# Turning and spreading the softmax sums by DMA instead of by small matrix products

## The chip, the cores and the metric

The kernel runs on one core of one Trainium2 chip. The metric is the device time of one execution in microseconds (us), lower is better. The core has a matrix engine (PE; its weight loads are listed as PEld), a vector engine (DVE), an activation engine (ACT), a general engine (POOL) and a sequencer (SP) that here issues nearly all the DMAs. Each engine executes its own instructions strictly in the order in which they were written, and waits on semaphores where it needs another engine's or a transfer's result.

## The reference, cut to what matters

Four layers are applied in turn to 4 images of 128 channels and 64 x 64 pixels, each with a group norm before it and a residual after it: self-attention, a 5x5 convolution, a two-directional selective scan (a state-space layer), and a 3x3 convolution. Only the attention is changed here:

```python
q = jnp.einsum('bnc,dc->bnd', xt, Wq) + bq
k = jnp.einsum('bnc,dc->bnd', xt, Wk) + bk
v = jnp.einsum('bnc,dc->bnd', xt, Wv) + bv
scores = jnp.einsum('bic,bjc->bij', q, k) * scale
attn = jax.nn.softmax(scores, axis=-1)
out = jnp.einsum('bij,bjc->bic', attn, v)
```

All of it is in f32. There are 4096 queries and 4096 keys to an image.

## The kernel before, in words

**Tiling of the attention.** `attention` (one image) holds the scores with keys on partitions and queries along the row. It takes 8 blocks of 512 queries (`NM`), and for each block 32 tiles of 128 keys (`NJT`): 256 steps u. Step u makes one score product (`scores`, L482), which ACT exponentiates into a ring of 8 slots (L488), and the value product of step u - 2 (`values`, L494), which accumulates 128 channels x 512 queries in a PSUM bank. An f32 product is two records in the profile. The softmax is normalised afterwards: each query's sum over all keys is needed, inverted, and then laid out 128 x 512, the same row on every partition, so that `settle` can multiply the raw output by it, add it to the residual and take the statistics of the next norm.

**The sums of a block.** In the images 1 to 3 (`sums`, L516) PE adds four ring slots at a time, each against a 128x32 block of ones in its own quarter of the PSUM bank "z"; ACT copies the bank out (`evict_sums`, L542). In image 0, which runs alone, PE makes no such products: DVE and POOL add the even and the odd tiles into two 128x512 tiles (`side_sums`, L536). ACT copies out the raw output (`evict`, L547).

**What is done with them.** Four functions follow, put into later steps by `after(u, n, f, blk)`. `turn` (L559), one step later, brings the sums of 512 queries from one row to a 128x4 column form by PE products with a one-column right side: four products where ACT's copy is the source, eight where the two side tiles are. `invert`, at 2 steps, copies the 128x4 to `zall` (which a check of range reads at the end) and takes the reciprocal on DVE (L568, L570). `widen_out`, at 4 steps, spreads the 128x4 to 128x512 by four products with the identity (`spread`, L474) into the bank "z". `settle`, at 5 steps, multiplies and adds on DVE (L582, L583) and has ACT take the squares (L331). The last block of an image does the same four at once, after the loop.

**The scan and its order.** The selective scan is cut into 1024 ticks, 256 to an image (`scan_core`). In each tick POOL makes the drive `db` (L1258, 128x1024); ACT exponentiates the decay `da` (L1251); DVE runs the recurrence (L1268) in two halves of 512 or in one of 1024; the weighting by `cr` is made by DVE (L1271) or, for two ticks in five while attention runs, by POOL (L1289); and PE collects the finished ticks by 128x32 products (L1309). SP loads `br`, `cr` (L1234) and every 32 ticks `de`, `dx` (L1228) four ticks ahead, into three buffers of each.

**How the two are woven.** Everything else is one long generator, `images`: the attention, the convolution and the scan's preparation of images 0, 1, 2, 3, and then the last parts of images 0 to 3. Image 0's attention and convolution run alone, with the constants of the convolution beside them. From then on the generator is advanced by the scan's loop. Each `yield` of the generator gives its price: 0.86 (`PRODUCT`) for each 512-column PE product, and some small constants for steps without. A tick hands out `PACE` = 2.8 of credit, half of it at each of two points, and the generator runs until it is spent. `turn` and `widen_out` cost one `PRODUCT` each. Thus scan of image b and attention and convolution of image b + 1 are laid side by side, and the pace decides how much of the second stands between two ticks. If image b + 1 isn't prepared when the scan of image b is out of ticks, `before` runs the generator without ticks until it is. During the last image's scan the pace is 1.5 (`ENDPACE`).

The engines' programs come out of this weaving: each function's instructions, DMAs on SP among them, are written where the generator calls it.

Of the kernel before, what the change touches and what calls it, by code (L numbers as in the profile page):

```python
# [24 lines left out]
F32 = mybir.dt.float32  # L25
I32 = mybir.dt.int32
AF = mybir.ActivationFunctionType
ALU = mybir.AluOpType
AX = mybir.AxisListType
# [3 lines left out]
P = 128  # L33
# [3 lines left out]
MM = 512  # L37
# [5 lines left out]

PRODUCT, HOP, SLOT, PACE, ENDPACE, AHEAD = 0.86, 1.7, 0.7, 2.8, 1.5, 4


BQ, BK, BX, BP, CONVB, BD, DSKIP, MAINB, CONVW, ALOG = 0, 1, 2, 3, 4, 5, 6, 7, 8, 12
# [3 lines left out]
def conv_preact_kernel(  # L53
# [16 lines left out]
    nc = tc.nc  # L70
# [8 lines left out]
    NJT = L // P  # L79
    NM = L // MM  # L80
    TPM = MM // P
# [6 lines left out]
    small = ctx.enter_context(tc.tile_pool(name="small", bufs=2))  # L88
    dram = ctx.enter_context(tc.tile_pool(name="dram", bufs=2, space=DRAM))
    ps = ctx.enter_context(tc.tile_pool(name="ps", bufs=1, space=PSUM))  # L90
    pools, ready = {}, set()
    more = None

    def bank(tag, name):
        return pools.get(tag, ps).tile([P, MM], F32, tag=tag, name=name)
# [22 lines left out]
    ones = const.tile([P, P], F32, name="ones")  # L118
# [52 lines left out]
    zall = const.tile([P, B * NJT], F32, name="zall")  # L171
# [265 lines left out]
    def attention(b, xs, xn, v, st, safe, loads):  # L437
# [3 lines left out]
        rq, acc, zp, mb = {}, {}, {}, {}  # L441
        N = NM * NJT

        def after(u, n, f, *args):
            later.setdefault(u + n, []).append((f, args))

        def queries(blk):
            pr = bank("s", f"pr_{b}_{blk}")
            nc.tensor.matmul(pr, wqk, xn[:, bass.ts(blk, MM)], start=True, stop=True)
            rq[blk] = pools["bg"].tile([P, MM], F32, tag="r", name=f"r_{b}_{blk}")  # L450
            nc.scalar.activation(rq[blk], pr, AF.Identity, bias=bqk)

        def row_max(blk):

            part = small.tile([P, TPM, NM], F32, tag="part", name=f"part_{b}_{blk}")
            for t in range(TPM):
                for k in range(NM):
                    pp = bank("s", f"pmax_{b}_{blk}_{t}_{k}")
                    nc.tensor.matmul(
                        pp, rq[blk][:, bass.ts(t, P)], xn[:, bass.ts(k, MM)],  # L460
                        start=True, stop=True,
                    )
                    nc.vector.tensor_reduce(part[:, t, k : k + 1], pp, AX.X, ALU.max)
            m = small.tile([P, TPM], F32, tag="rmax", name=f"rmax_{b}_{blk}")
            nc.vector.tensor_reduce(m, part, AX.X, ALU.max)
            pb = bank("s", f"pmb_{b}_{blk}")
            spread(pb, m)
            mb[blk] = pools["bg"].tile([P, MM], F32, tag="w", bufs=4, name=f"mb_{b}_{blk}")
            nc.scalar.copy(mb[blk], pb)
# [9 lines left out]
        def scores(u):  # L479
            blk, j = divmod(u, NJT)  # L480
            sc = bank(("s", "s2")[u % 2], f"sc_{b}_{u}")
            nc.tensor.matmul(sc, xn[:, bass.ts(j, P)], rq[blk], start=True, stop=True)  # L482
            pt = ring[:, u % NRING, :]
            if safe:
                nc.vector.tensor_tensor(pt, sc, mb[blk], ALU.subtract)
                nc.scalar.activation(pt, pt, AF.Exp)
            else:
                nc.scalar.activation(pt, sc, AF.Exp)  # L488

        def values(u):  # L490
            blk, j = divmod(u, NJT)
            if j == 0:
                acc[blk] = bank("a", f"acc_{b}_{blk}")
            nc.tensor.matmul(  # L494
                acc[blk], v[:, j, :], ring[:, u % NRING, :], start=j == 0, stop=j == NJT - 1
            )
# [5 lines left out]
        def sums_due(u):  # L502
            beside = "collected" in ready
            ready.discard("collected")
            if due and due[0][1] <= u and (beside or u >= due[0][2]):
                sums(due.pop(0)[0])
                return PRODUCT
            return 0.0

        def sums(u):  # L510

            blk, j = divmod(u, NJT)
            if j == 3:
                zp[blk] = bank("z", f"zp_{b}_{blk}")
            for g in range(4):
                nc.tensor.matmul(  # L516
                    zp[blk][g * 32 : (g + 1) * 32, :], ones[:, :32],
                    ring[:, (u - 3 + g) % NRING, :], start=j == 3, stop=j == NJT - 1,
                    tile_position=(0, g * 32), skip_group_check=True,
                )  # L520

        state = {}


        fill = pools.get("fill") if not safe else None
        sides = {}

        def side_sums(u):
            blk, j = divmod(u, NJT)
            eng, e = (nc.vector, nc.gpsimd)[j % 2], "dp"[j % 2]  # L530
            if j < 2:
                sides[blk, e] = fill.tile([P, MM], F32, tag=f"side{e}", name=f"side{e}_{blk}")
                eng.tensor_copy(sides[blk, e], ring[:, u % NRING, :])
            else:
                s = sides[blk, e]
                eng.tensor_tensor(s, s, ring[:, u % NRING, :], ALU.add)  # L536

        def evict_sums(blk):
            zs = None
            if not fill:  # L540
                zs = pools["bg"].tile([P, MM], F32, tag="zs", bufs=1, name=f"zs_{b}_{blk}")
                nc.scalar.copy(zs, zp.pop(blk))  # L542
            state[blk] = None, zs

        def evict(blk):
            raw = pools["bg"].tile([P, MM], F32, tag="raw", bufs=1, name=f"raw_{b}_{blk}")
            nc.scalar.copy(raw, acc.pop(blk))  # L547
            state[blk] = raw, state[blk][1]
# [44 lines left out]
        for u in range(N):  # L593
            blk, j = divmod(u, NJT)
            cost = sums_due(u)
            if safe and j == 0:
                row_max(blk)
            scores(u)
            cost += PRODUCT

            if j == 17 and blk + 1 < NM:
                queries(blk + 1)
                cost += PRODUCT
            w = u - 2
            if w >= 0:
                if w < N - HELD:
                    values(w)
                    cost += PRODUCT
                d = w % NJT
                if fill:  # L610
                    side_sums(w)
                elif d == NJT - 1:
                    sums(w)
                    cost += PRODUCT
                elif d % 4 == 3:
                    due.append((w, u + (3 if d == 3 else 1), u + NRING - 5))
                if d == NJT - 1:
                    evict_sums(blk - 1)
                    evict(blk - 1)
                    for n, f in ((1, turn), (2, invert), (4, widen_out), (5, settle)):  # L620
                        after(u, n, f, blk - 1)
            for f, args in later.pop(u, ()):
                f(*args)
                cost += PRODUCT if f in (turn, widen_out) else 0.0
            next(loads, None)
            yield cost or HOP
        for w in (N - 2, N - 1) if fill else ():
            side_sums(w)
        blk = NM - 1
# [16 lines left out]
        if not fill:  # L646
            sums(N - 1)
            yield PRODUCT
        taps_to(NRING - 4)
        evict_sums(blk)  # L650
        values(N - 3)
        taps_to(NRING - 3)
# [727 lines left out]
    def program(safe):  # L1380
# [24 lines left out]
        def front(b, xn, v):  # L1405

            xs = large(b + 1, f"xs_{b}")[:, :L]
            st = Sums(f"e{b}")
            yield from attention(b, xs, xn, v, st, safe, load(xs, b))
            st2 = Sums(f"s{b}")  # L1410

            yield from conv_pairs(b, xs, f"A{b % 2}", st, st2, b > 0 or safe)
            if b + 1 == B:
                nc.sync.dma_start(m3, main_w)

            def mat(name):
                return dram.tile([NCH, P, CH], F32, tag=name, name=f"{name}_{b}")

            mats4[b] = (
                [mat("bm"), mat("cm")], mat("dd"), mat("dxd"), mat("xcd"),  # L1420
                dram.tile([P, L], F32, tag="xsd", bufs=B, name=f"xsd_{b}"),
            )
            ynds[b] = dram.tile([NM, P, MM], F32, tag="ynd", bufs=B, name=f"ynd_{b}")
            operands = yield from scan_prep(b, xs, st2, mats4[b])
            if b + 1 < B:
                return (yield from both(operands, start(b + 1, 10)))
            yield from operands
            last_weights()
# [225 lines left out]
```

## Time and profile before

| | |
|---|---|
| time, median of 3 (lowest to highest) | 4425.42 us (4424.64 to 4433.18) |
| span of the profiled execution | 4424.0 us |
| busy: PE, DVE, POOL, ACT | 3917.4, 3698.5, 3602.1, 2358.3 us |
| image 0's attention alone | about 30 to 490 us |
| image 0's convolution and scan preparation | about 490 to 684 us |
| scan of image 0 beside attention of image 1 | about 730 to 1363 us |
| scan of image 0 beside convolution, preparation of image 1 | about 1363 to 1633 us |
| the same for images 1 and 2 | 1664 to 2299 and on to 2572; 2609 to 3242 and on to 3511 us |
| scan of image 3 beside the last parts of images 0 to 2 | about 3511 to 4350 us |

The profiled execution's own time isn't recorded apart from its span, which is 1.4 us under the median of the timed runs, and 0.6 us under the fastest. In a table of stretches, each engine's figure is its busy time in that stretch with the count of its instructions in brackets, then the TensorE clock granted, the DMA share and the rate. In a group's line stand the code line, the engine, the operation, what it writes and reads, the count, then busy time in us and the mean of one in ns, then the idle time just before them and what ended it. A busy PE is not PE at its peak: ends of products are modelled, and a product that starts every 429 ns is shown as 592 ns long.

### The profile page before, as it was taken

What the parts mean: (1) busy time and instruction counts of PE and PEld (TensorE: products, weight loads), DVE (VectorE), ACT (ScalarE), POOL (GpSimd) and SP (SyncE); (2) the same over time, 40 slices, a digit from 0 to 9 for tenths busy, and PEclk for the clock granted to TensorE, in tenths of its full rate; (3) what the DMA queues carried; (4) which work ended last, traced back from release to release, by engine and by line L of the source; (5) the groups of instructions that cost most, each with busy time, mean ns of one, the idle gap of its engine ahead of it and who ended that gap; (6) DMA issues with size and microseconds to landing.
All of it is one profiled execution on the core that took longest, in us unless ns stands there. A gap on an engine that the chain in (4) does not pass through costs nothing. (4 is left out here: it accounts for less than half of the span.)

```text
span 4424.0 us, 43050 instructions
## 1 busy us (share of the span) xinstructions
PE 3917.4 (89%) x13480; PEld 1485.9 (34%) x13480; DVE 3698.5 (84%) x3472; ACT 2358.3 (53%) x4269; POOL 3602.1 (81%) x1713
## 2 busy tenths in 40 slices
PE   8999997999999979999989889999989748575667
PEld 4444433333333323333333333333333212121212
DVE  4722217999999989999999889999999899999996
ACT  3333217666665376666664576666653744454533
POOL 3433307999999978999999889999989889999995
PEclk9999999999999989999999989999999869787888
DMA  1000016545455566554544564454545665656562
GB/s 64 21 1 1 0 53 228 182 170 175 168 186 180 179 214 212 177 175 174 180 164 180 205 231 177 165 179 173 180 175 182 226 228 193 232 202 235 187 226 84
DMA packets 213167, 726.06 MB, mean 164 GB/s; under 512 B 25152, under 2 KB 26432, under 8 KB 212672
## 3 DMA queue, kind: packets, MB, share of 16 engines
q1 hardware_dynamic: 211328, 722.49, 46.3%
q8 instruction: 108, 1.77, 0.2%
q14 instruction: 131, 1.07, 0.1%
q10 hardware_dynamic: 1600, 0.73, 0.1%
HBM read 653.98 MB, written 69.14 MB: 163 GB/s over the span
## 5 line engine op out<-in xcount | busy, mean ns | idle before, releaser
L1258 POOL TENSOR_TENSOR db<-dx,br 128x1024 f32<-128x1024 f32 x1024 | 2398.1, 2365 | 223.8 <-DMA dx<-dxd 55.6
L1251 ACT ACTIVATE da<-de,a_neg 128x512 f32<-128x512 f32 (+1 forms) x1640 | 1302.4, 797 | 740.6 <-DVE da L1268 300.5
L482 PE MATMUL sc<-r,x 128*128 128x512 f32 x2048 | 1078.6, 609 | 14.8 <-ACT last L1284 6.9
L494 PE MATMUL acc<-exchange,v 128*128 128x512 f32 x2048 | 1048.3, 594 | 2.3
L1289 POOL TENSOR_TENSOR hc<-hc,cr 128x1024 f32<-128x1024 f32 x386 | 913.0, 2365 | 22.5 <-ACT last L1284 19.7
L1271 DVE TENSOR_TENSOR hc<-da,cr 128x512 f32<-128x512 f32 (+1 forms) x1003 | 839.6, 837 | 65.0 <-DVE da L1268 0.5
L1268 DVE TENSOR_TENSOR_SCAN da<-da,last,db 128x512 f32<-128x512 f32 (+1 forms) x480 | 863.1, 1798 | 24.3 <-POOL db L1258 12.1
L488 ACT ACTIVATE exchange<-sc 128x512 f32<-128x512 f32 x1024 | 603.5, 589 | 510.4 <-PE sc L482 503.9
L1309 PE MATMUL y<-hc,sel 128*32 128x512 f32 x4096 | 611.9, 647 | 270.6 <-POOL hc L1289 245.3
L482 PEld LDWEIGHTS sc<-r,x 128*128 128x128 f32 x2048 | 361.3, 190 | 585.6 <-issue 379.2
L494 PEld LDWEIGHTS acc<-exchange,v 128*128 128x128 f32 x2048 | 386.4, 190 | 499.2 <-issue 478.0
L1268 DVE TENSOR_TENSOR_SCAN hc<-da,last,db 128x512 f32<-128x512 f32 (+1 forms) x288 | 490.9, 1704 | 6.5 <-ACT da L1251 5.2
L1268 DVE TENSOR_TENSOR_SCAN da<-da,da,db 128x512 f32<-128x512 f32 x365 | 469.7, 1287 | 6.2 <-ACT da L1251 5.9
L536 POOL TENSOR_TENSOR sidep<-sidep,exchange 128x512 f32<-128x512 f32 x120 | 170.7, 1422 | 273.5 <-ACT exchange L488 271.3
L1268 DVE TENSOR_TENSOR_SCAN hc<-da,hc,db 128x512 f32<-128x512 f32 x251 | 322.0, 1283 | 35.6 <-ACT da L1251 11.8
L1309 PEld LDWEIGHTS y<-hc,sel 128*32 128x32 f32 x4096 | 114.4, 113 | 706.1 <-POOL hc L1289 337.7
L536 DVE TENSOR_TENSOR sided<-sided,exchange 128x512 f32<-128x512 f32 x120 | 95.9, 799 | 221.5 <-ACT exchange L488 220.1
L1268 DVE TENSOR_TENSOR_SCAN da<-da,db 128x512 f32<-128x512 f32 (+1 forms) x158 | 232.5, 1471 | 15.5 <-POOL db L1258 7.1
L698 PE MATMUL pcm<-xpm,cs 128*128 128x512 f32 x432 | 210.1, 635 | 23.1 <-ACT xpm L387 23.1
L964 PE MATMUL pe<-df,exchange 128*128 128x512 f32 x480 | 214.2, 595 | 0.0
L516 PE MATMUL zp<-exchange,ones 128*32 128x512 f32 x1536 | 204.9, 600 | 8.3 <-DVE xs L583 8.3
L1284 ACT COPY last<-da 128x1 f32<-128x1 f32 x474 | 73.8, 156 | 254.5 <-DVE hc L1271 252.0
(241 smaller groups left out, 2839.1 us busy)
## 6 DMA issues: line engine op xcount, KB each, us to landing
br<-bm SPq DMA_DIRECT2D x512, 512.0 KB, 5.2
cr<-cm SPq DMA_DIRECT2D x512, 512.0 KB, 3.9
de<-dd SPq DMA_DIRECT2D x64, 512.0 KB, 4.7
dx<-dxd SPq DMA_DIRECT2D x64, 512.0 KB, 6.2
x<-in_x_dram SPq DMA_DIRECT2D x16, 512.0 KB, 5.9
xs<-in_x_dram SPq DMA_DIRECT2D x16, 512.0 KB, 6.1
xsd<-xs SPq DMA_DIRECT2D x16, 512.0 KB, 6.0
xcd<-xc SPq DMA_DIRECT2D x16, 512.0 KB, 2.8
```

The lines of the kernel that those rows point to most:

```text
L482: nc.tensor.matmul(sc, xn[:, bass.ts(j, P)], rq[blk], start=True, stop=True)
L488: nc.scalar.activation(pt, sc, AF.Exp)
L494: nc.tensor.matmul(acc[blk], v[:, j, :], ring[:, u % NRING, :], start=j == 0, stop=j == NJT - 1)
L536: eng.tensor_tensor(s, s, ring[:, u % NRING, :], ALU.add)
L698: nc.tensor.matmul(acc.rearrange("p (r w) -> p r w", w=W), weights[:, t, :], xp[:, y : y + RPM, dx : dx + W], start=t == 0, stop=t == k * ...
L964: nc.tensor.matmul(flat(acc), matrix(w, dx), view(r, dx), start=k == 1, stop=k == total and (n == 0 or not lean),)
L1251: nc.scalar.activation(da, rep["de", b, c, d, g][:, bass.ts(h, size)], AF.Exp, scale=a_neg[:, at(i)])
L1258: nc.gpsimd.tensor_tensor(dbs[i], rep["dx", b, c, d, g], rows["b", b, c, d, q], ALU.mult)
L1268: nc.vector.tensor_tensor_scan(h, da, db[:, cut], before, ALU.mult, ALU.add)
L1271: nc.vector.tensor_tensor(hc[:, cut], h, rows["c", b, c, d, q][:, cut], ALU.mult)
L1289: nc.gpsimd.tensor_tensor(hcs[i], hcs[i], rows["c", b, c, d, q], ALU.mult)
L1309: nc.tensor.matmul(y[r : r + SG, :], sel, hcs[first + gg][:, bass.ts(h, MM)], start=q == back, stop=False, tile_position=(0, r), skip_grou ...
```

## The change

For every block but an image's last, `turn`, `invert` and `widen_out` are replaced by a path through DRAM. `spill` writes the sums' rows (four of them; two in image 0) to DRAM, `gather` reads them back as 128 partitions x rows x 4, `invert_rows` adds the rows into `zall` and takes the reciprocal of 128x4, `put_rows` writes that to DRAM, and `fetch_rows` reads it to all 128 partitions as 128x512 in SBUF. They stand at 2, 4, 7, 9 and 11 steps after the block, and `settle` at 15 instead of 5. All four transfers are issued by SP. In image 0 the two side tiles are first summed over partitions by two PE products with 128x32 ones, at the end of the block, and ACT copies 64 x 512 out. Since `turn` and `widen_out` leave the loop, their price of two `PRODUCT` to a block leaves the credit count too (image 0 counts one, but runs outside the credit). `PACE` is 2.76 instead of 2.8. An image's last block keeps the old path.

```diff
-PRODUCT, HOP, SLOT, PACE, ENDPACE, AHEAD = 0.86, 1.7, 0.7, 2.8, 1.5, 4
+PRODUCT, HOP, SLOT, PACE, ENDPACE, AHEAD = 0.86, 1.7, 0.7, 2.76, 1.5, 4
...
                 nc.scalar.copy(zs, zp.pop(blk))
+            elif blk + 1 < NM:
+                zs = pools["bg"].tile([P, MM], F32, tag="zs", bufs=1, name=f"zs_{b}_{blk}")
+                pz = bank("z", f"pz_{b}_{blk}")
+                for g, e in enumerate("dp"):
+                    nc.tensor.matmul(
+                        pz[g * 32 : (g + 1) * 32, :], ones[:, :32], sides.pop((blk, e)),
+                        start=True, stop=True, tile_position=(0, g * 32), skip_group_check=True,
+                    )
+                nc.scalar.copy(zs[:64], pz[:64])
             state[blk] = None, zs
+
+        RUN = MM // P
+
+        def spill(blk):
+            raw, zs = state[blk]
+            n = 2 if fill else 4
+            zd = dram.tile([4, MM], F32, tag="zp", name=f"zd_{b}_{blk}")
+            nc.sync.dma_start(zd[:n], zs[0 : n * 32 : 32, :])
+            state[blk] = raw, zd[:n]
+
+        def gather(blk):
+            raw, zd = state[blk]
+            zt = small.tile([P, 4, RUN], F32, tag="zt", name=f"zt_{b}_{blk}")
+            n = zd.shape[0]
+            nc.sync.dma_start(zt[:, :n, :], zd.rearrange("g (p j) -> p g j", j=RUN))
+            state[blk] = raw, zt[:, :n, :]
+
+        def invert_rows(blk):
+            raw, zt = state[blk]
+            z = zall[:, b * NJT + blk * TPM : b * NJT + (blk + 1) * TPM]
+            nc.vector.tensor_reduce(z, zt.rearrange("p g j -> p j g"), AX.X, ALU.add)
+            zr = small.tile([P, RUN], F32, tag="zr", name=f"zr_{b}_{blk}")
+            nc.vector.reciprocal(zr, z)
+            state[blk] = raw, zr
+
+        def put_rows(blk):
+            raw, zr = state[blk]
+            zd = dram.tile([P, RUN], F32, tag="zd", name=f"zd_{b}_{blk}")
+            nc.sync.dma_start(zd, zr)
+            state[blk] = raw, zd
+
+        def fetch_rows(blk):
+            raw, zd = state[blk]
+            rb = pools["bg"].tile([P, MM], F32, tag="rb", bufs=1, name=f"rb_{b}_{blk}")
+            row = zd.rearrange("p j -> (p j)").unsqueeze(0)
+            nc.sync.dma_start(rb, row.to_broadcast([P, MM]))
+            state[blk] = raw, rb
...
-                    for n, f in ((1, turn), (2, invert), (4, widen_out), (5, settle)):
+                    for n, f in (
+                        (2, spill), (4, gather), (7, invert_rows),
+                        (9, put_rows), (11, fetch_rows), (15, settle),
+                    ):
                         after(u, n, f, blk - 1)
+                    cost += PRODUCT if fill else 0.0
             for f, args in later.pop(u, ()):
                 f(*args)
-                cost += PRODUCT if f in (turn, widen_out) else 0.0
```

## The prediction

> **What bounds the kernel now.** I read the table of stretches first, because shares over the whole span mix stages.
>
> ```profile
> 30.00:490.00 460.00, 460.00 (x1198) 212.34 (x1197) 180.59 (x229) 165.82 (x283) 173.18 (x126) 1.00 0.01 6
> 730.00:1363.00 633.00, 622.36 (x2377) 232.98 (x2378) 599.13 (x616) 407.26 (x840) 594.72 (x257) 1.00 0.51 179
> 1363.00:1500.00 137.00, 127.80 (x417) 50.50 (x417) 127.70 (x99) 58.47 (x73) 129.64 (x66) 0.96 0.54 188
> 1500.00:1633.00 133.00, 116.78 (x411) 40.65 (x413) 111.26 (x116) 74.84 (x112) 99.39 (x51) 0.94 0.56 199
> 3511.00:4350.00 839.00, 538.77 (x1674) 155.83 (x1666) 808.85 (x489) 399.65 (x637) 802.27 (x363) 0.79 0.61 216
> ```
>
> Image 0's attention is PE alone: 460.0 of 460 us. Beside the scan PE (98%), DVE (95%) and POOL (94%) are all nearly full. In the last stretch DVE and POOL bound and the change touches nothing there (no attention, `ENDPACE` kept). So the middle is the question. Next, who waits, in 730 to 1363 us, engine by engine (DVE, POOL, PE):
>
> ```profile
> DVE da L1268 <- POOL db L1258: 5.4, 7, 1.5
> DVE hc L1268 <- ACT da L1251: 3.7, 8, 0.9
> DVE da L1268 <- ACT da L1251: 2.8, 3, 1.6
> DVE hc L1268 <- POOL db L1258: 0.9, 2, 0.7
> ...
> POOL db L1258 <- DMA dx<-dxd: 19.4, 5, 7.8
> POOL db L1258 <- DVE hc L1268: 6.9, 8, 1.7
> ...
> PE zp L516 <- DVE xs L583: 4.2, 6, 1.3
> ```
>
> DVE waits for only some 13 us of 633; its other idle time is short gaps between instructions. PE waits for about 10. Both run flat out, coupled through ACT, which serves the exponentials of both. So a shorter PE can save at most about what DVE still waits. Last, the groups that go, image 0's attention first, then 800 to 1300 us:
>
> ```profile
> L559 PE MATMUL pz<-ones,sidep 128*128 128x1 f32 x56 | 10.1, 250 | 0.0
> L559 PE MATMUL pz<-ones,sided 128*128 128x1 f32 x56 | 9.5, 240 | 0.0
> L474 PE MATMUL pzb<-ident,zr 128*128 128x128 f32 x56 | 7.4, 275 | 0.0
> ...
> L1258 POOL TENSOR_TENSOR db<-dx,br 128x1024 f32<-128x1024 f32 x144 | 337.3, 2363 | 32.9 <-DMA dx<-dxd 19.4 <-DVE hc L1268 5.3 <-PE sc L482 2.4
> L482 PE MATMUL sc<-r,x 128*128 128x512 f32 x400 | 212.2, 612 | 1.7 <-ACT last L1284 1.5
> ```
>
> 144 ticks in 500 us: 3.47 us a tick. 200 steps (two records each): 2.5 us a step, 1.39 steps a tick.
>
> **Image 0.** From the timeline at 206.73 to 208.44 us, a `turn` holds PE for 16 records at 0.112 us, 1.71 to 1.79 us; a `widen_out` (213.67 to 214.56) for 0.89. Removed: 2.68 us a block. Added: two products of 512 columns into different column groups. The scan's collecting products (L1309), four groups at once, show two passes at 0.429 us, so 0.86. Also added is an order: ACT copies the sums out (L542's 585 ns) ahead of the raw output (586 ns), and the next block's first value product waits for the latter. Now the copy at 205.13 to 205.72 ends just before that product at 205.79. After, PE ends the sums at about 205.95, ACT both copies at about 207.25, and PE, with one score product between, is ready at 206.65: 0.6 us of wait, behind which all of PE's queue stands. Net -2.68 + 0.86 + 0.65 = -1.17 us a block, 7 blocks: -8.2. Once, near 146 us, DVE's last side addition is held up by a constant of the convolution (2774 ns, then the addition until 147.57), where PE now stands at 146.2: +1.4. Sum -7. It is on the path: PE is 100% busy there and nothing else sets the stage's end. The two DVE operations (163 + 178 ns) are replaced by a 16-element reduction and the same reciprocal, hidden by DVE's 279 us of idle time.
>
> **Images 1 to 3.** `turn` is 8 records at 0.112, 0.89 us, and `widen_out` 0.89: with 7 blocks, 12.5 us of PE work an image, against a price of 2 x 0.86 x 7 = 12.0 that leaves the credit count. PE's waits for `settle` to free the bank "z" (4.2 us here, 11 of them for 8.3 us over the three) go too, since ACT's copy now frees it. Does anything shift against the scan? Attention costs 256 x 1.72 + 64 x 0.86 + 7 x 0.86 (the next queries) + 12 = 513 of credit, 183 ticks at 2.8 (the trace: 633 us at 3.47, 182); after, 501 at 2.76, 182 ticks. The whole image had 716.8 to spend and has 706.6, 10.2 less for 12.0 less work, so the next image is ready at the same tick or slightly earlier, and the steps forced without ticks don't grow (-1 us).
>
> The floor of the gain is 0: DVE sets every tick. The ceiling is 15 us an image, 46 in all: every saved PE microsecond counts (12.5 + 2.8). I take 5 in each attention, below half, as DVE's 13 us of waits are the nearest row and about half of them (`da` from ACT, 6.5) can come from PE through ACT. In the convolution and preparation, 270 us and some 74 ticks an image, the lower pace takes 74 x 0.04 = 3 us of PE work; DVE is busy for only 239 of the 270 there, so I take 2. Together -21, and -1.
>
> **What the DMAs cost.** Each block puts four transfers in SP's queue, 84 in the middle images. `spill` waits for ACT's copy (2 steps, 5 us old), `gather` for the landing of `spill`, `put_rows` for DVE's reciprocal (2 steps old), `fetch_rows` for the landing of `put_rows`. Behind each in SP's queue stand `br` and `cr` loads. These are the rows that say what such a hold costs:
>
> ```profile
> SPq L1234 <- POOL hc L1289: 290.2, 69, 11.0
> SPq L1234 <- DVE hc L1271: 152.1, 50, 6.5
> SPq L1337 <- ACT ys L1335: 23.5, 5, 8.7
> ...
> br<-bm SPq DMA_DIRECT2D x512, 512.0 KB, 5.2
> dx<-dxd SPq DMA_DIRECT2D x64, 512.0 KB, 6.2
> ynd<-ys SPq DMA_DIRECT2D x62, 128.0 KB, 2.3
> ```
>
> SP waits most of the time for a `cr` buffer anyway (442 us of 633), and the store of `ys`, which waits for ACT right after it is issued, holds it up 4.7 us at a time without any wait for `br` in POOL's list. A landing wait should be 2.3 (the nearest row by size, `ynd`) to 5.2 us (`br`); the trace has no transfer in pieces of 16 bytes like `gather`'s 512, and I keep 5.2 for it. 2 steps have passed by then, 5 us. So nearly all of it hides behind the buffer waits. Not hidden are `de` and `dx`, whose loads POOL already waits for (19.4 us); in the changed program's order a new transfer stands just ahead of them at two blocks of seven. I take +1 us an image, between 0 and 2 x 2.3. DVE waits for `gather` 3 steps (7.5 us) after its issue and for `fetch_rows` 4 steps after: covered, and if it weren't, the recurrences would stand behind it. `settle` reads SBUF in place of PSUM: 680 ns against 692 for L1271 with an SBUF operand, +2 us in all at most.
>
> The Trainium skill, "DMA: Bandwidth & Descriptors", section "Rules for kernel authors", speaks against this: a transpose by a plain DMA with a rearranged access pattern is given as 19 times slower than the hardware's, and transfers under 64 KB as mostly overhead. Its "Anatomy of one DMA" puts the fixed part at about 2.0 us. Were all four on the path, that page's 8 us a block would make 168 us over 21 blocks, and the kernel some 140 us slower; the `ynd` row's 2.3 agrees with the fixed part, but I take it as hidden, as above.
>
> **Sum**, against the span of 4424.0: -7 - 15 - 6 - 1 + 3 + 2 = -24, span 4400. The median stands 1.4 above the profiled span: 4401.
>
> **Rivals.** (A) DVE holds every tick, and only image 0 gains: 4425 - 7 = 4418. For it: DVE's 13 us of waits in 633. Against: PE's own 622 busy, and PE at 93% in the convolution. (B) All PE work saved counts: 4425 - 7 - 46 = 4372. For it: ACT idles longest for DVE and for the score product alike, so PE is as often last; against, the same 13 us. (C) Slower: `gather` or `put_rows` blocks SP's queue, `br` and `dx` land late, POOL's `db` is late and DVE stands behind it. If a block costs 1.8 us so, 21 blocks give 38, and 4425 - 7 + 38 = 4456 with no gain left in the middle; it decides from 1.1 us a block (24 / 21), which is half a landing. For it: 20-odd `dx` loads are waited for now. Against: the `ys` stores. (D) The transfers could be so late that `settle` is held, which would show in DVE; 15 steps, 37 us, for four transfers of at most 5.2 and two waits of 2 steps make it unlikely, and I count it with C.
>
> **How the numbers follow.** No change that this kernel's measurement can tell is within 0.2%, 8.9 us: 4416.6 to 4434.3. Chances: the forecast 0.48 (4385 to 4414), A 0.19, B 0.17 (about 4362 to 4385), C 0.16 (4434 and up, some of it just below). A third of A lies under 4416.6, so faster 0.48 + 0.17 + 0.06 = 0.71; same 0.14, slower 0.15. The range reaches to B's 4372 and, for part of C, to 4432; some 0.08 lies below and 0.12 above. The faster cases' own range is 4372 to 4415.
>
> **What would show it.** Image 0: its attention ends about 7 us earlier, with ACT's raw copy ending waits of PE of about 0.6 us a block. Middle: attention of 626 to 630 us, no `zp` wait for `xs`, SP waits of a few us on the new lines, DVE waits under 13 us. Wrong would be: POOL's waits for `br` or `dx` up by over 10 us an image (C), or an attention stretch of 633 (A) or of 618 (B), or a forced stretch before a scan.

## The result, and the profile after

The changed kernel takes 4501.17 us (median of 4) against 4427.08 before: 1.0164 times as long, 95% interval 1.0152 to 1.0175. The prediction was 4401, between 4372 and 4432. It was wrong in sign. The ratios further down are each to the kernel before as it ran in the same round (4428.9 to 4429.4 us).

Where the time lies can be read off the first POOL drive of each image's scan (L1258 before, L1307 after), in us from the span's start:

| | scan of image 0 begins | image 0's scan | image 1's | image 2's | image 3's scan to the end | span |
|---|---|---|---|---|---|---|
| before | 684.0 | 949.1 | 939.4 | 939.0 | 912.4 | 4424.0 |
| after | 679.2 | 982.8 | 964.3 | 962.9 | 911.4 | 4500.6 |
| difference | -4.8 | +33.7 | +24.9 | +23.9 | -1.0 | +76.6 |

Image 0, alone on PE, became faster as forecast. All the loss, 82 us, lies in the scans of the images 0 to 2, beside which the next image's attention, convolution and preparation run. From the first to the last score product of each image (L482), the three attentions take 1966 us where they took 1904, 62 more; the rest of the three scans takes 945 where it took 924, 21 more. Those 21 go with the new path's credit count: attention now takes 540 ticks of the scan, not 546, and six ticks of 3.5 us come to lie outside it. In every run below that has the new path and the pace of 2.76 the rest is 944 to 951 us, whether its `settle` is slow or not; in every run with the old path beside the scan it is 924 to 928. The table of stretches of the kernel after (image 0's attention; attention of image 1 beside the scan; its convolution; its preparation; the last scan):

```profile
30.00:488.00 458.00, 453.97 (x1064) 195.37 (x1063) 175.60 (x229) 169.11 (x292) 174.41 (x127) 1.00 0.04 10
726.00:1387.00 661.00, 627.98 (x2274) 225.28 (x2275) 615.23 (x611) 404.19 (x835) 593.65 (x255) 0.97 0.51 172
1387.00:1525.00 138.00, 124.84 (x402) 49.22 (x401) 123.50 (x95) 55.31 (x70) 124.93 (x65) 0.95 0.54 186
1525.00:1662.00 137.00, 115.51 (x403) 40.91 (x402) 119.43 (x121) 78.19 (x116) 109.79 (x55) 0.95 0.58 206
3589.00:4425.00 836.00, 524.80 (x1653) 157.69 (x1656) 806.33 (x481) 394.02 (x627) 799.30 (x362) 0.78 0.62 215
```

Attention of image 1 takes 661 us where it took 633. PE has 103 records fewer, but DVE, with 5 instructions fewer, is busy for 615 us where it was 599. Two lines of DVE's groups carry that. First `settle` beside the scan in the kernel before (730 to 1363 us):

```profile
L583 DVE SCALAR_TENSOR_TENSOR xs<-pzb,bv_c,xs 128x512 f32<-128x512 f32 x7 | 5.3, 751 | 0.2
L582 DVE TENSOR_TENSOR pzb<-raw,pzb 128x512 f32<-128x512 f32 x7 | 4.8, 679 | 0.0
```

the same two operations after (726 to 1386 us):

```profile
L629 DVE SCALAR_TENSOR_TENSOR xs<-rb,bv_c,xs 128x512 f32<-128x512 f32 x7 | 15.3, 2182 | 0.2
L628 DVE TENSOR_TENSOR rb<-raw,rb 128x512 f32<-128x512 f32 x7 | 14.1, 2021 | 0.0
```

and after, in image 0's attention, where POOL is idle for more than half of the time:

```profile
L629 DVE SCALAR_TENSOR_TENSOR xs<-rb,bv_c,xs 128x512 f32<-128x512 f32 x7 | 5.3, 752 | 0.3
L628 DVE TENSOR_TENSOR rb<-raw,rb 128x512 f32<-128x512 f32 x7 | 4.8, 683 | 0.0
```

Same instruction, same sizes, three times as long beside the scan. What differs from before is only where the reciprocals lie: in a PSUM bank (`pzb`) then, in SBUF (`rb`) now, so that each operation reads two SBUF tiles. The timeline of DVE and then of POOL around one of them (start, duration) shows what it does in that time:

```profile
927.06 2.74 DVE L628 TENSOR_TENSOR rb<-raw,rb 128x512 f32<-128x512 f32 x1
929.84 2.91 DVE L629 SCALAR_TENSOR_TENSOR xs<-rb,bv_c,xs 128x512 f32<-128x512 f32 x1
932.68 0.08 DVE L629 DVE_READ_ACCUMULATOR xs<-rb,bv_c,xs 128x1 f32 x1
```

```profile
926.90 2.35 POOL L1338 TENSOR_TENSOR hc<-hc,cr 128x1024 f32<-128x1024 f32 x1
929.86 2.34 POOL L1307 TENSOR_TENSOR db<-dx,br 128x1024 f32<-128x1024 f32 x1 [0.61 <-DVE rb L628]
```

POOL's operation ends at 929.25 and DVE's 0.55 us later, at 929.80; POOL's next ends at 932.20 and DVE's second 0.55 us later, at 932.75. DVE stands until POOL's operation is done and then takes its own half microsecond. (In the second pair DVE's record starts 0.02 us ahead of POOL's, and it is still DVE that waits; starts this close don't tell which was first.) It also goes the other way: at 2773.80 DVE's `rb` starts first and takes 0.67 us, and the POOL operation that started 0.18 us after it takes 2.69 instead of 2.36.

It is so throughout. Of the 42 operations of `settle` in the 21 blocks beside the scan, 34 end 0.55 us after the end of a POOL operation; the other 8 began with no POOL operation under way and took 0.67 or 0.75 us. Two POOL operations that start during one of DVE's are again waited for; the other 22 that do end 2.20 to 2.23 us after DVE's end and take 2.64 to 2.82 us. Before, with `pzb` in PSUM, none of the 64 operations of `settle` takes more than 0.75 us, whatever POOL does. The weightings of the scan (L1271 before), 692 ns beside the same POOL, also have one of their two inputs in PSUM.

The Trainium skill has this on the page "SBUF — State Buffer". Section "Who interferes with whom" says that a DVE instruction with two SBUF inputs contends with a GpSimd (POOL) instruction that reads SBUF, and that a DVE instruction with at most one SBUF input, outside the two-port modes, doesn't contend. Section "SBUF: two separate sides" says that whichever of the two starts first gets the shared pair of ports for the whole instruction, and the other is blocked. The numbers above agree with all three: 34 of 42 operations held until POOL was done, none of the 64 with an operand in PSUM. The runs below test it.

Then there is a second effect, in PE's waits in the same attention (none of these was longer than 1.5 us before):

```profile
PE sc L482 <- ACT r L451: 19.6, 5, 6.3
PE sc L482 <- ACT last L1333: 10.9, 2, 6.5
```

In six of the seven blocks of image 1 PE stands for 3.1 to 6.5 us. `settle` now comes at 15 steps, one step ahead of the next block's query product (`queries` at j = 17), whose PSUM bank "s" is one of the two that the scores use. ACT's squares wait for DVE's long `settle`:

```profile
932.79 0.72 ACT L331 ACTIVATE junk<-xs,aw_e 128x512 bf16<-128x512 f32 x1 [4.74 <-DVE xs L629]
...
936.41 0.68 ACT L451 ACTIVATE r<-pr,bqk 128x512 f32<-128x512 f32 x1
```

and only behind them, in ACT's order, is the query bank emptied, which PE's score waits for: `[6.30 <-ACT r L451]` before the product at 937.14. Around the end of each of these six stalls the granted clock is 0.50 for 3.4 or 6.8 us, and the mean over the attention is 0.97 instead of 1.00.

### The profile page after: what moved, and what is told of

It reads as the page before. It is cut to its first block, busy times and chain, and to the rows that moved or that the text cites. A ratio compares the mean times of both kernels' runs of the same rounds, so it can differ in the third digit from the quotient of the medians.

```text
span 4500.6 us, 42269 instructions
## 1 busy us (share of the span) xinstructions
PE 3906.8 (87%) x13004; PEld 1444.8 (32%) x13004; DVE 3744.0 (83%) x3453; ACT 2353.9 (52%) x4270; POOL 3625.0 (81%) x1718
## 5 line engine op out<-in xcount | busy, mean ns | idle before, releaser
L1307 POOL TENSOR_TENSOR db<-dx,br 128x1024 f32<-128x1024 f32 x1024 | 2407.3, 2372 | 272.8 <-DVE hc L1317 66.7
L482 PE MATMUL sc<-r,x 128*128 128x512 f32 x2048 | 1101.6, 621 | 89.2 <-ACT r L451 48.6
L494 PE MATMUL acc<-exchange,v 128*128 128x512 f32 x2048 | 1062.8, 601 | 3.8 <-ACT last L1333 0.8
L1338 POOL TENSOR_TENSOR hc<-hc,cr 128x1024 f32<-128x1024 f32 x391 | 924.7, 2365 | 35.6 <-ACT last L1333 33.1
L1358 PE MATMUL y<-hc,sel 128*32 128x512 f32 x4096 | 595.5, 645 | 267.3 <-POOL hc L1338 255.9
L482 PEld LDWEIGHTS sc<-r,x 128*128 128x128 f32 x2048 | 371.7, 193 | 695.2 <-issue 400.3
L1317 DVE TENSOR_TENSOR_SCAN hc<-da,last,db 128x512 f32<-128x512 f32 (+1 forms) x294 | 500.7, 1703 | 8.9 <-ACT da L1300 5.6
L1317 DVE TENSOR_TENSOR_SCAN da<-da,da,db 128x512 f32<-128x512 f32 x357 | 459.5, 1287 | 18.1 <-ACT da L1300 17.9
L536 POOL TENSOR_TENSOR sidep<-sidep,exchange 128x512 f32<-128x512 f32 x120 | 169.0, 1409 | 268.5 <-ACT exchange L488 266.4
L536 DVE TENSOR_TENSOR sided<-sided,exchange 128x512 f32<-128x512 f32 x120 | 94.0, 783 | 264.1 <-ACT exchange L488 263.5
```

The source lines that it names most:

```text
L494: nc.tensor.matmul(acc[blk], v[:, j, :], ring[:, u % NRING, :], start=j == 0, stop=j == NJT - 1)
L1307: nc.gpsimd.tensor_tensor(dbs[i], rep["dx", b, c, d, g], rows["b", b, c, d, q], ALU.mult)
L1317: nc.vector.tensor_tensor_scan(h, da, db[:, cut], before, ALU.mult, ALU.add)
L1338: nc.gpsimd.tensor_tensor(hcs[i], hcs[i], rows["c", b, c, d, q], ALU.mult)
L1358: nc.tensor.matmul(y[r : r + SG, :], sel, hcs[first + gg][:, bass.ts(h, MM)], start=q == back, stop=False, tile_position=(0, r), skip_grou ...
```

## The experiments

The rivals that the runs were to part: **P**, DVE and POOL wait for each other in `settle`; **Q**, the new neighbourhood of `settle` and the query product; **S**, the transfers and SP's queue; and the pace.

**Only the operand.** The kernel before with the reciprocals copied to SBUF:

```diff
+        def lift(blk):
+            if fill:
+                return
+            raw, pb = state[blk]
+            rb = pools["bg"].tile([P, MM], F32, tag="rb", bufs=1, name=f"rb_{b}_{blk}")
+            nc.scalar.copy(rb, pb)
+            state[blk] = raw, rb
...
-                    for n, f in ((1, turn), (2, invert), (4, widen_out), (5, settle)):
+                    for n, f in ((1, turn), (2, invert), (4, widen_out), (5, lift), (6, settle)):
```

> The kernel before, with one step put in: at 5 steps ACT copies the spread reciprocals out of PSUM into SBUF, and at 6 the two DVE operations of settle read them there (images 1 to 3, all blocks but the last). No transfers, no change of pace. Theory P (the DVE operations of settle, which now read two SBUF tiles each, have to wait for POOL's operation that runs at the time): in the profile after they take 2021 and 2182 ns beside the scan where they took 679 and 751 before, 2.8 us more a block and 58 us over 21 blocks, and POOL's operations that meet them are 2.8 us long, not 2.36; so this kernel should be 50 to 90 us slower than before, at 4475 to 4515, with the same long durations. Theory Q (settle at 15 steps has come to stand just ahead of the next block's query product at 17, and ACT's squares, which wait for settle, hold up r and with it PE): settle isn't near the query product here, so no more than 15 us slower, 4425 to 4440. Theory S (the transfers hold up SP): no transfers, so the same as Q.

Its control ends `lift` with `state[blk] = raw, pb`:

> The control of the run before: the same copy by ACT at 5 steps and settle at 6, but settle goes on reading PSUM and nothing reads the copy. All theories: the copy is 0.59 us of ACT a block, 12 us over 21 blocks on an engine that is busy for 64%, so 0 to 10 us slower than before, 4425 to 4435, and settle's two operations stay at about 680 and 751 ns.

Measured: 4487.8 us (1.0131 of before, 1.0115 to 1.0148) and, for the control, 4434.8 (1.0014, 1.0004 to 1.0023). The groups of `settle` in the first, over the whole span, then in the control between 800 and 1300 us:

```profile
L591 DVE SCALAR_TENSOR_TENSOR xs<-rb,bv_c,xs 128x512 f32<-128x512 f32 x21 | 43.4, 2066 | 0.7
L590 DVE TENSOR_TENSOR rb<-raw,rb 128x512 f32<-128x512 f32 x21 | 42.3, 2013 | 1.1 <-ACT rb L584 1.1
```

```profile
L591 DVE SCALAR_TENSOR_TENSOR xs<-pzb,bv_c,xs 128x512 f32<-128x512 f32 x6 | 4.5, 751 | 0.2
L590 DVE TENSOR_TENSOR pzb<-raw,pzb 128x512 f32<-128x512 f32 x6 | 4.1, 688 | 0.7 <-ACT rb L584 0.7
```

The one difference between the two kernels is the memory in which `settle` has the reciprocals, and it is worth 53 us. The DVE time explains it almost to the microsecond: (2.013 + 2.066 - 0.688 - 0.751) x 21 = 55 us. P holds, without any transfer, pace or step of the change.

**Only the neighbourhood.** The query product moved away from `settle` in the changed kernel, and moved next to it in the kernel before:

```diff
# after
-            if j == 17 and blk + 1 < NM:
+            if j == 25 and blk + 1 < NM:
# before
-            if j == 17 and blk + 1 < NM:
+            if j == 7 and blk + 1 < NM:
```

> The changed kernel with the next block's query product at 25 instead of 17, nine steps behind settle. Theory Q: the waits of PE's scores for r or last (2 to 6.5 us, once a block) go, and with them most of the loss; 4400 to 4430. Theory P: DVE and POOL still lose 60 us to each other, PE's long wait only gets shorter since two score banks are then free; 4470 to 4500, settle's operations still 2.0 and 2.2 us.

> The kernel before with the query product at 7 instead of 17, just behind its own settle at 6: the same neighbourhood as in the changed kernel, with settle's operands in PSUM. Theory Q: one wait of PE for r of some us a block and 40 to 80 us slower than before, 4465 to 4505. Theory P: settle is short here, so 0 to 20 us slower, 4425 to 4445.

Measured: 4477.9 (1.0106 of before, 1.0090 to 1.0123) and 4429.6 (1.0001, 0.9991 to 1.0010). Moving it away wins 23 us back, and PE's waits for `r` are gone from its list (its two longest entries, in 730 to 1380 us):

```profile
PE sc L482 <- ACT exchange L488: 15.8, 9, 4.7
PE sc L482 <- ACT last L1333: 4.9, 3, 2.9
```

Moving it next to a short `settle` costs nothing that can be told (4 us either way). So Q alone isn't the cause; it is a second price of the same long operations, about 23 of the 74 us. Image 0 pays perhaps a little of it too: its scan begins at 675.7 us with the query product at 25, against 679.2 after and 684.0 before. But the five other runs below that have this very program for image 0 begin their scan at 676.0 to 678.5 us, so this is 1 to 4 us.

**Only image 0, and only the transfers.** The first keeps the old path, with its pace and prices, unless `fill` is set (image 0); the second issues the four transfers for 21 blocks beside the old path, unread:

```diff
# image 0 alone
+                    for n, f in (
+                        (2, spill), (4, gather), (7, invert_rows),
+                        (9, put_rows), (11, fetch_rows), (15, settle),
+                    ) if fill else ((1, turn), (2, invert), (4, widen_out), (5, settle)):
...
+            if j == (25 if fill else 17) and blk + 1 < NM:
# transfers beside
+                    for n, f in (
+                        (1, turn), *(() if fill else ((2, spill),)), (2, invert), (4, widen_out),
+                        (5, settle), *(() if fill else ((4, gather), (9, put_rows), (11, fetch_rows))),
+                    ):
```

> The kernel before with the new path in image 0 alone (its query product at 25, so that it doesn't stand just behind settle); images 1 to 3 and the pace as before. In the profile after, image 0's scan began 4.8 us earlier than before with the query product at 17, and 8.3 us earlier with it at 25. POOL is idle for more than half of that stage, so settle from SBUF costs nothing there (683 and 752 ns). So 5 to 9 us faster than before, about 4420. If the order of the scan behind it swallows the gain: the same as before.

> The kernel before with the four transfers of the new path put beside the old one for 21 blocks of images 1 to 3 (at 2, 4, 9 and 11 steps, the same sizes and pieces), and nothing reading what they bring. Theory S (the transfers and SP's waits for them cost time): 20 to 40 us slower. Theory P (the loss is DVE and POOL waiting for each other in settle): 0 to 6 us slower, though SP's list shows some 25 us of waits for the landings per attention.

Measured: 4423.4 (0.9986 of before, 0.9977 to 0.9995) and 4429.1 (0.9999, 0.9990 to 1.0009). Image 0's path is a gain of about 6 us (2 to 10). The transfers cost nothing that can be told (4 us either way), far from the 20 to 40 of S. SP does wait for their landings (first list, 730 to 1363 us), and POOL's waits for these loads stay what they were, 19.0 us in sum against 19.4 before (`dx` alone then):

```profile
SPq L1261 <- POOL hc L1316: 274.9, 69, 8.4
SPq L1261 <- DVE hc L1298: 120.5, 45, 6.5
...
SPq L590 <- DMA zd<-zs: 14.4, 5, 4.6
...
SPq L601 <- DMA ze<-zr: 11.5, 4, 3.7
```

```profile
POOL db L1285 <- DMA dx<-dxd: 15.0, 4, 4.9
...
POOL db L1285 <- DMA br<-bm: 4.0, 4, 1.4
```

What SP waits there it no longer waits for a `cr` buffer (395 us against 442). S falls. The landings that this run's profile gives, 6.0 us for `gather` and 7.4 for `put_rows` (medians), are longer than the 5.2 at most of the prediction, and hide all the same.

**The conflict taken away.** With the reciprocals in SBUF, POOL can do `settle`'s work itself, and then has nobody to wait for:

```diff
+        def weigh_out(blk):
+            raw, rb = state[blk]
+            cut = bass.ts(blk, MM)
+            nc.gpsimd.tensor_tensor(rb, raw, rb, ALU.mult)
+            nc.gpsimd.tensor_tensor(xs[:, cut], rb, xs[:, cut], ALU.add)
+            ready.add("weighed")
+
+        def finish(blk):
+            state.pop(blk)
+            cut = bass.ts(blk, MM)
+            nc.scalar.activation(
+                xs[:, cut], xs[:, cut], AF.Identity, bias=bv_c, accum_out=st.sum(blk)
+            )
+            st.squares(blk, xs[:, cut], xs[:, 0:1])
...
-                        (9, put_rows), (11, fetch_rows), (15, settle),
+                        (9, put_rows), (11, fetch_rows),
+                        *(((15, settle),) if fill else ((15, weigh_out), (19, finish))),
...
+                if pooled[i] and "weighed" in ready:
+                    pooled[i] = False
+                    ready.discard("weighed")
```

with the query product at 25. The unbalanced form drops `"weighed"` and the last three lines, so that POOL keeps all its weightings.

> The changed kernel with settle of images 1 to 3 (but the last block) taken from DVE: POOL multiplies and adds at 15 steps (two operations of 128x512, about 1.27 us each), ACT adds the bias with the sum and takes the squares at 19, and for each such block one weighting by cr (2.37 us) goes from POOL to DVE, so that both have about the load of the kernel before; the query product is at 25. No DVE operation with two SBUF tiles is left beside the scan but in the last blocks. Theory P: the loss goes, 4390 to 4425, with image 0's 8 us and whatever PE's 12.5 us an image are worth when DVE and POOL have their old load: if DVE sets each tick, nothing more (4415 to 4420); if every us of PE counts, 4380. Were the transfers or the pace at fault: 4450 or more.

> The same without the shift of a weighting to DVE: POOL has 2.5 us a block more than before (53 us over 21 blocks, against some 38 us that it waits in each attention), DVE 1.4 less. If DVE sets the ticks: faster than the run before, 4390 to 4415; if POOL does: slower than it by up to 40 us.

Measured: 4425.6 (0.9988 of before, 0.9979 to 0.9997) and 4411.2 (0.9958, 0.9942 to 0.9973). The whole loss is gone. POOL's two operations have 512 columns where `db` has 1024, and take a little over half of its 2.36 us, in the unbalanced run:

```profile
L628 POOL TENSOR_TENSOR rb<-raw,rb 128x512 f32<-128x512 f32 x21 | 26.9, 1281 | 0.0
L629 POOL TENSOR_TENSOR xs<-rb,xs 128x512 f32<-128x512 f32 x21 | 26.8, 1275 | 1.6
```

Its attention beside the scan:

```profile
727.00:1346.00 619.00, 614.85 (x2274) 220.82 (x2275) 586.33 (x591) 410.42 (x848) 605.81 (x268) 1.00 0.55 183
```

619 us where it was 633, with POOL up from 595 to 606 us and DVE down from 599 to 586. That isn't all gain: over the three images attention takes 538 ticks instead of 546 and is 35 us shorter, and the rest of the scans is 24 us longer, so that the three scans gain 12. (The expectation is wrong on one point: the last blocks read PSUM, and twelve DVE operations on two SBUF tiles stay beside the scan in the preparation, 1.9 to 2.0 us each in the mean.)

The balanced form, in which DVE and POOL have the old load and PE 12.5 us an image less, gains no more than image 0's own path did: the PE work taken away bought nothing there. With DVE's load taken down 14 us more came, so DVE set the ticks. The unbalanced form beats both kernels.

**What PE's products were worth.** The unbalanced form with the small products, and the pace of 2.8, put back (`lift` at 5, `weigh_out` at 15, `finish` at 19, no transfers):

> The kernel before, small PE products and pace of 2.8 kept, with settle on POOL as in the unbalanced run: ACT copies the spread reciprocals to SBUF at 5 steps, POOL multiplies and adds at 15, ACT adds the bias and squares at 19, the query product at 25 (images 1 to 3, all blocks but the last). No transfers. Against the unbalanced run this puts back PE's 12.5 us an image and image 0's old path. If DVE sets the ticks, PE's products are worth nothing beside the scan, and only image 0's 5 to 8 us are lost: 4414 to 4422. If PE's work counts in full, 45 us are lost: 4450 to 4460.

Measured: 4421.8 (0.9985 of before, 0.9976 to 0.9993), 10.6 us behind the unbalanced run (13.9 between the profiled executions). Image 0 is 9.2 of the latter (its scan begins at 686.4 against 677.2); the three scans beside attention take 2821 us against 2816. So 37 us of PE work, and PE's waits for the bank "z", were worth some 5 us, which single profiles don't tell from nothing: the kernel before and the one with the new path in image 0 alone have the same program beside the scan, and take 2828 and 2834.

The length of a tick, from drive to drive over the three attentions, says the same. It is 3.474 us before (3.469 to 3.480 in the four runs that differ least from it) and 3.640 after; 3.582 and 3.477 in the operand pair; 3.592 after with the query product at 25; 3.493 in the balanced form; and, with `settle` unbalanced on POOL, 3.463 without the small products and 3.462 with them. At some 540 ticks the operand is worth 57 us, its meeting with the query product 26, and the small products nothing that shows.

**One operation of two.** Multiplication on POOL at 14, the addition on DVE at 15, query product at 25:

> The changed kernel with only the multiplication of settle on POOL (at 14 steps); the addition to the residual stays on DVE with two SBUF tiles (at 15), the query product at 25. Theory P: half of what lies between the run with queries at 25 (4478) and the unbalanced run (4411): 4435 to 4455, the remaining DVE operation still 2.1 us or so.

Measured: 4461.7 (1.0080 of before, 1.0065 to 1.0094), a miss by 7 us. The remaining operation is as long as expected, but has a new wait, now for POOL itself (whole span):

```profile
L632 DVE SCALAR_TENSOR_TENSOR xs<-rb,bv_c,xs 128x512 f32<-128x512 f32 x21 | 46.6, 2221 | 24.4 <-POOL rb L627 20.1 <-DMA cr<-cm 4.3
```

24 us of idle DVE before this operation, where the run at 25 has 1; half the operations moved is less than half the gain.

**The pace.**

```diff
-PRODUCT, HOP, SLOT, PACE, ENDPACE, AHEAD = 0.86, 1.7, 0.7, 2.76, 1.5, 4
+PRODUCT, HOP, SLOT, PACE, ENDPACE, AHEAD = 0.86, 1.7, 0.7, 2.8, 1.5, 4
```

> The changed kernel with the pace put back to 2.8, all else as changed. If the lower pace had any part in the loss, this is faster than 4501 by over 10 us; under theory P, with DVE setting the ticks, 4490 to 4510, and attention takes two or three ticks fewer.

> The unbalanced run (settle on POOL, transfers, queries at 25) with the pace put back to 2.8. If PE still limits some ticks there, slower than 4411 by 3 to 10 us; if DVE and POOL alone set them, the same within 5 us.

Measured: 4489.0 for the changed kernel at 2.8 (1.0140 of before, 1.0125 to 1.0155; 12 faster than at 2.76, so that the lower pace did have this part in the loss) and 4422.0 for the unbalanced one (0.9983, 0.9974 to 0.9991; 11 slower than at 2.76). At the higher pace the scan of image 3 up to its last drive takes 820 us instead of 835, and 823 instead of 836 in the unbalanced form, since more of the other work has been done by then: DVE has 462 instructions there instead of 481. The three scans before it pay for that: 26 us in the unbalanced form, 2 in the changed kernel. So the pace was a trade of some 12 us, one way in the one kernel and the other way in the other. In the unbalanced form a tick of attention takes 3.476 us at 2.8 and 3.463 at 2.76, 7 of the 26 us, so that PE may still limit some ticks there, as its expectation has it; the other 19 lie outside attention. Why the changed kernel pays only 2 isn't settled here.

**What adds up.** 53 us for the operand, 23 for the query product beside it and -6 for image 0, each from its own pair of runs, make 70 of the 74 us; the products and the transfers are within their noise of 0.

## Why the prediction was wrong

**The step that failed** is one sentence of the part on the DMAs: "`settle` reads SBUF in place of PSUM: 680 ns against 692 for L1271 with an SBUF operand, +2 us in all at most". L1271 reads one SBUF tile and one PSUM tile; `settle` now reads two SBUF tiles beside a POOL that is 94% busy with operations of 2.36 us. Measured: 2.0 and 2.2 us in image 1's attention, 2.8 us more a block there and 2.6 over all 21 blocks, and 53 us in the pair of runs that differ in nothing else.

The trace of before held rows that fit. This one (of all of DVE's groups, over the whole span) is an operation on two SBUF tiles of the same size, in the preparation beside the scan:

```profile
L1112 DVE TENSOR_TENSOR exchange<-exchange,u 128x512 f32<-128x512 f32 x12 | 18.5, 1602 | 4.2 <-ACT u L1136 4.2
```

Five of the twelve took 2.82 or 2.83 us and one 0.97, each ending 0.55 us after a POOL operation; the other six took 0.68 to 0.70. Priced by this mean against 0.69, two operations in each of 21 blocks would have come to 38 us more (an estimate), and the forecast to a slower kernel. In image 0, too, 14 of DVE's 120 side additions (L536, two SBUF tiles, mostly 0.69 us) took 1.09 to 1.75 and ended 0.55 us after a POOL operation. The prediction used one of these, at 146.48 us, for its wait, not for its duration.

**What the reading of the waits was for.** "A shorter PE can save at most about what DVE still waits" was right, and it should have turned the question round: with 13 us of waits in 633, nearly every microsecond added to DVE must be a microsecond of the kernel. 55 us of it added 53.

**Image 0**: right in mechanism; -7 forecast, -4.8 measured, and -5.5 to -8.3 in the six runs with the query product out of the way. (The sum has 0.65 us a block for a wait that it had worked out as 0.6; that is 0.4 us in all.) The wait for `r` (3.7 us in three places) was not foreseen, the wait for ACT's raw copy didn't show.

**Images 1 to 3**: -22 was too much, even without the conflict. The products are worth 0 to 5 of their 46 us, near rival A's 0. That taking half of DVE's waits away would shorten the stage was a guess, and it wasn't so: in the balanced form DVE's waits for `da` from ACT in image 1's attention are 2.7 us instead of 6.5, and a tick is no shorter than before (3.493 us against 3.474). The -6 for the convolution and preparation was wrong in sign: the scans' part outside attention became 21 us longer.

**The credit count** kept the next image in time, as worked out: the longest pause between two drives around the end of an image's scan was 26, 17 and 19 us before, and 24, 16 and 14 after. The last scan is as long as before (911.4 us against 912.4), as said; but at 2.8 it is 896.5, and the sum had no term for what the lower pace gave away there.

**The transfers**: +3 forecast, 0 measured (-0.1 to +0.1%, or 4 us either way, so that 3 isn't excluded); rival C, the one that ended on this side, had the wrong mechanism. The landings hide behind SP's buffer waits, as argued. The section that the prediction cites for 2.0 us describes DMAs issued by POOL, while these four are SP's.

**The step numbers**: `settle` at 15 was placed by its own data and its buffers, and the sum has no term for what stands at 17, behind it in ACT's order: 23 us, once `settle` had become long.

## What to carry to other kernels

When a change moves a DVE operand from PSUM to SBUF, count the SBUF inputs of each DVE instruction: with two of them beside a busy POOL, the price is the wait for POOL's operation, not the instruction's own time, and a row with the same shape but a PSUM operand says nothing about it. Where two engines are both full, find the one that a run shows to set the pace (here DVE, which waited for 13 us in 633) and price the change on that one first. And when an instruction moves to a later step, look at what it now stands ahead of on every in-order engine that waits for it.

## What the runs showed of the hardware

- A DVE operation on two SBUF tiles of 128x512 takes 0.67 to 0.75 us alone and up to 2.9 us (4.45 once, across two POOL operations) beside POOL operations on SBUF; it then ends 0.55 us after POOL's. A POOL operation of 128x1024 (2.36 us) that starts while DVE's is under way ends 2.20 us after it and takes 2.64 to 2.82 us. With one of the two inputs in PSUM, DVE's takes 0.67 to 0.75 us beside the same POOL.
- Four small transfers a block, one of them in 512 pieces of 16 bytes, cost nothing measurable (4 us either way in 4429) beside a stream of 180 GB/s, with SP waiting 26 us for their landings in one attention.
- Of 18 PE stalls of 2.3 to 6.5 us in the three attentions of the changed kernel, 16 had a stretch of 3.4 or 6.8 us at a granted clock of 0.50 around their end (two of 2.3 us had none). Products that start every 0.43 us start every 0.85 there, so a stall cost more than its length.
